# Attention logits, exponentials and the byte mask of a two-layer graph network: from VectorE by tiles to ScalarE by heads, with other positions of the steps

## The chip, the core and the metric

The kernel runs on one core of one Trainium2 chip. The metric is the device time of one execution in microseconds (us); less is better. The engines are TensorE (PE, with its weight loads PEld), VectorE (DVE), ScalarE (ACT), GpSimd (POOL) and SyncE (SP), which here issues every DMA. Each engine has its own queue of instructions, in the order in which the program gives them; between engines, semaphores make one wait for another.

## What is computed

```python
# layer 0: 12 heads of 64, 128 graphs of 64 nodes, 768 features
h = einsum('bnd,ade->bane', x, W);  th = tanh(h)
attn = (th @ w_src) + swapaxes(th @ w_dst, 2, 3)
attn = where(attn >= 0, attn, 0.2 * attn)          # the leaky unit
attn = softmax(where(~adj, -999.0, attn), axis=-1)
f = elu(attn @ h + b);  gate = sigmoid(x @ H_w.T + H_b)
x = layernorm(x + gate * f + (1 - gate) * x)
# layer 1: 6 heads of 128, masked softmax attention with Wq, Wk, Wv, Wf
x = layernorm(x + attention(x, adj))
```

All is float32; the adjacency is bytes.

## The kernel before

**Tiles and pairs.** The 8192 nodes are 64 tiles of 128 rows (two graphs each), worked on in 32 pairs. Of a pair, `t1` is the second tile and `t0` the first; keys in the tables of positions end in 1 or 0 for them.

**Items.** Layer 0 is one long list of items, and each item is one product on PE. `a0` to `a14` are the fifteen products (L925) by which a pair's features and gate are made (a fast matrix multiplication with fifteen in place of eighteen block products, each of two chunks and 512 columns). `v1` to `v7` are the seven products of layer 1's values (L962), one pair behind; written `u` they belong to the pair before that. From the fifth pair on every pair has the same 22 items, the table `TURN`; such a stretch is called a turn here. The first four pairs have their own tables `EARLY`, and `LAST` ends the phase.

**Ways out.** A product adds into a bank of PSUM, its path (`PRODUCTS`, L49). A path is used by several products, and the bank is read between them: `step` (L369) first gives PE the product and then writes out the product before it (`way_out`, L948), either by a copy or a negation on ACT where a block of `hg` is written for the first time, or by an addition on DVE. The next product of the same path has to wait until that read is done: a12 uses the same path as a10, with one item between them, and a14 the same as a12.

**Positions.** All other work is entered in a plan at positions counted in items (the tables `NEW`, `SUMS` and `OLD`, those with `EARLY` for the first four pairs). After each item the plan's steps of that position are emitted in order of their positions (L1344 to L1350). `behind_of` (L1263) counts from the last of some of the pair's products, `was` (L1257) from the beginning of the next turn for the tile's later steps, `at` (L1260) from the beginning of the pair's own turn. The product a7 stands at item 11 of a turn, a14 at 17, a12 at 15, before and after. So a position on an engine is only its place in that engine's queue.

**The steps of one tile's attention**, in order:

- `products` (L975, key tanh): tanh on ACT, then th times the two vectors on DVE (L980) and POOL (L981)
- `terms` (L984): the sums over 64 features on DVE (L989), giving `sd`, 24 numbers a row; a transpose on DVE (L994)
- `send` (L997) and `fetch` (L1000): the transposed terms go to DRAM and come back as `dd`, spread over the rows of each graph; SP issues one DMA and then two
- `with_bias`, `other_half` (L1009, L1016; keys bias and hx): a bias on POOL, two DMAs that swap the halves
- `logits` (L1023): one DVE addition over 128x768 with `sd` spread over the columns; `leaky` (L1034): one ACT instruction over 128x768
- `masked` (L1038): DVE replaces masked places by -999 (L1042), takes each head's maximum (L1048) and subtracts it (L1049)
- `exps` (L1051): one ACT instruction over 128x768, which writes the heads in the order in which PE turns them
- `probs_by_nodes` (L1069, key probs): PE turns prob into two banks, ACT copies them out (L1067)
- `attend` (L1080): 48 small products, `av`; `features` (L1096): reciprocals and products on DVE, then an exponential on ACT (L1111)
- `elu1`, `gated` (L1119, L1124): three DVE operations, the last at L1130; `stats`, `power`, `normed`: the layernorm's sums on DVE, the root on POOL, the result on ACT

`mask` (L1176) makes, once a pair, bytes that are 1 where there is no edge. `gate_bias` on POOL (L1185) and `gate_tanh` on ACT (L1187) prepare the gate, and `residual` (L1114) multiplies on POOL. `x_sums` (L868) makes the next operands on POOL.

**Weights.** Products read their weights from slots of `wa`, one a product. While the last pair runs, slots that are done with are filled with layer 1's weights for queries and keys (`load_wide`, L447); `wide_place` (L438) says which slot, by the constant `ORDER`, which lists the products in the order in which `TURN` uses them. From the fourth pair to the last, one more stream of DMAs and POOL operations makes sums of layer 1's weights (`sum_weights`, L410).

**Layer 1** (L1361 on) has its own loops and is not touched by the change.

Of the kernel before, what the change touches and what calls it, by code (L numbers as in the profile page):

```python
# [16 lines left out]
P = 128  # L17
N = 64
# [53 lines left out]
ORDER = (0, 1, 5, 3, 8, 6, 7, 2, 10, 9, 12, 4, 14, 11, 13)  # L72
# [60 lines left out]
TURN = "u6 a0 a1 u5 u7 a5 a3 u4 u3 a8 a6 a7 a2 a10 a9 a12 a4 a14 a11 v1 a13 v2".split()  # L133

EARLY = (
    "a0 a5 a1 a7 a3 a8 a6 a10 a9 a2 a12 a4 a11 a14 a13".split(),
    "a0 a5 a3 a7 a8 a6 a1 a9 a10 a2 a12 a4 a11 a14 a13".split(),
    "a0 a1 a3 a5 a8 a6 a7 u1 u2 u6 u5 u7 a10 u4 a2 a9 a12 a11 a4 a14 a13 u3".split(),
# [4 lines left out]
NEW = dict(tanh1=1, terms1=3.3, bias1=3.7, send1=6.3, hx1=4.6, fetch1=6.5, logits1=8.5, leaky1=10.5,  # L143
    masked1=10.8, exps1=11, tanh0=1.6, terms0=3.3, bias0=3.4, send0=4.2, hx0=6.8, fetch0=4.6,
    gbias0=3.7, gbias1=2.8)
SUMS = dict(next6=2.1, next9=0.4, next2=2, next3=2.6, next0=2.7, next5=9.9, next8=5.9, own10=4.3, own12=5.8,
    own13=1.6)
OLD = dict(probs1=4.7, gtanh1=1.7, resid1=3.2, attend1=5.3, feat1=5.5, elu1=6, gated1=7.7, stats1=8.2, pow1=9,
    norm1=10.6, byf1=12.3, spill1=13.7, logits0=1.3, leaky0=2.5, masked0=3.6, exps0=5, gtanh0=6.9,
    resid0=7.7, probs0=7.8, attend0=10.5, feat0=11, elu0=12, gated0=13.8, stats0=14, pow0=14.9,  # L150
    norm0=16.6, byf0=17.3, spill0=20.7, sum0=17.9, sum1=18.3, sum2=23, sum3=28, spillT=21.5, spillV=12,
    mask=7.7, adj=6.4, xT=2.7, inputs1=0.8, inputs0=17.3, plus1=13.7, plus0=19.7)
OLD_EARLY = [
    dict(probs1=1.5, gtanh1=0, resid1=2.5, attend1=3, feat1=4.7, elu1=6, gated1=6.1, stats1=7, pow1=8,
        norm1=9.3, byf1=10, spill1=13, logits0=3, leaky0=4.3, masked0=5, exps0=5.7, gtanh0=4.5,
        resid0=5.8, probs0=8, attend0=11, feat0=12, elu0=12.2, gated0=13.6, stats0=14, pow0=15,
        norm0=15.5, byf0=17.5, spill0=18, sum0=10.4, sum1=18, sum2=20.7, sum3=26.9, spillT=19,
        spillV=11, mask=6, adj=3, xT=-2, inputs1=9.2, inputs0=14.5, plus1=14.9, plus0=17.5),
    dict(probs1=-3.3, gtanh1=1, resid1=1.5, attend1=3, feat1=4.7, elu1=5.7, gated1=7.1, stats1=7.3,
        pow1=8, norm1=9, byf1=11.3, spill1=11.7, logits0=2.5, leaky0=4, masked0=5, exps0=6.3,  # L160
        gtanh0=2.2, resid0=6.8, probs0=8, attend0=10, feat0=10.5, elu0=12, gated0=12.4, stats0=13,
        pow0=14, norm0=16, byf0=17, spill0=22.5, sum0=12, sum1=18, sum2=22, sum3=23.7, spillT=19.5,
        spillV=13, mask=6.5, adj=5.2, xT=-3, inputs1=10.5, inputs0=12.7, plus1=14.3, plus0=15),
    dict(probs1=2.5, gtanh1=1, resid1=3.5, attend1=4.5, feat1=5, elu1=6, gated1=6.1, stats1=9, pow1=9.5,
        norm1=11, byf1=11.3, spill1=12, logits0=1.7, leaky0=4.6, masked0=5, exps0=6, gtanh0=1.5,
        resid0=2.1, probs0=8.3, attend0=10, feat0=11, elu0=11.7, gated0=13.1, stats0=13.3, pow0=14,
        norm0=15, byf0=16.3, spill0=17, sum0=12, sum1=18, sum2=20.5, sum3=21, spillT=19, spillV=14,
        mask=4, adj=-0.3, xT=-0.6, inputs1=10.5, inputs0=13.2, plus1=13.7, plus0=17),
    dict(probs1=1.5, gtanh1=1, resid1=2, attend1=3.5, feat1=4.5, elu1=6, gated1=6.1, stats1=6.7, pow1=8,
        norm1=9, byf1=10, spill1=12.3, logits0=3, leaky0=4, masked0=4.5, exps0=6.5, gtanh0=1.7,  # L170
        resid0=5.7, probs0=8, attend0=9, feat0=10, elu0=12, gated0=12.1, stats0=14, pow0=15, norm0=16,
        byf0=17, spill0=19, sum0=11, sum1=18.5, sum2=22, sum3=23, spillT=18.5, spillV=11.6, mask=8.2,
        adj=2.5, xT=1.3, inputs1=13, inputs0=12, plus1=14.6, plus0=16.7),
]
NEW_EARLY = [
    dict(tanh1=1, terms1=2, bias1=3.1, send1=3.5, hx1=5.3, fetch1=6, logits1=8, leaky1=9, masked1=10,
        exps1=12, tanh0=1.3, terms0=2.5, bias0=3.1, send0=4, hx0=4.7, fetch0=5.7, gbias0=1, gbias1=1.5),
    dict(tanh1=1, terms1=3, bias1=2.5, send1=4, hx1=4.5, fetch1=4.5, logits1=8.3, leaky1=9.5,
        masked1=10, exps1=10.5, tanh0=2, terms0=3.2, bias0=2.9, send0=4.6, hx0=3, fetch0=7.5, gbias0=1,
        gbias1=7),  # L180
    dict(tanh1=1, terms1=2, bias1=4.6, send1=3.8, hx1=7, fetch1=6, logits1=7.7, leaky1=9.3,
        masked1=10.3, exps1=11, tanh0=1, terms0=2, bias0=3.1, send0=4.2, hx0=7.5, fetch0=9.5, gbias0=1,
        gbias1=1.6),
    dict(tanh1=1.3, terms1=3, bias1=3.6, send1=4, hx1=5, fetch1=4.5, logits1=8, leaky1=8.4, masked1=9.7,
        exps1=10.5, tanh0=1, terms0=2.2, bias0=6.4, send0=4, hx0=7, fetch0=6.3, gbias0=1.3, gbias1=1.3),
]
SUMS_EARLY = [
    dict(next6=0, next9=1.1, next2=1.5, next3=1.6, next0=4.9, next5=2.5, next8=1, own10=1.5, own12=0.9,
        own13=1),
    dict(next6=1.3, next9=0.1, next2=0.9, next3=1.6, next0=3.4, next5=0.8, next8=0.5, own10=2,  # L190
        own12=2.6, own13=1.5),
    dict(next6=0.8, next9=1.1, next2=2.2, next3=2.3, next0=3.6, next5=1.5, next8=3, own10=2.1,
        own12=0.1, own13=1),
    dict(next6=1, next9=1.1, next2=1.2, next3=1.3, next0=1.4, next5=1.5, next8=2.7, own10=1, own12=3.1,
# [5 lines left out]
def kernel(  # L200
# [236 lines left out]

    def wide_place(key, n):  # L438
        if key == "f":
            flat, at = weights[key].rearrange("p b k f -> p (b k f)"), PLACE[n]  # L440
        else:
            i = n + (key == "k") * NW
            flat, at = weights["a"].rearrange("p b k f -> p (b k f)"), 2 * ORDER[i // 2] + i % 2
        at = at * 2 * W2
        return flat[:, at : at + 2 * W2].rearrange("p (k f) -> p k f", k=2)
# [373 lines left out]
    with ExitStack() as ph, ExitStack() as ph_r:  # L819
# [203 lines left out]
        def logits(t):  # L1023
            sd, dd = st[t].pop("sd"), st[t].pop("dd")
            att = work(f"att_{t}")
            V.tensor_tensor(  # L1026
                att.rearrange("p (a c m) -> p a c m", c=2, m=32),
                dd.rearrange("p (c a m) -> p a c m", c=2, m=32),
                sd[:, H0 : 2 * H0].unsqueeze(2).unsqueeze(3).to_broadcast([P, H0, 2, 32]),
                ALU.add,  # L1030
            )
            st[t]["att"] = att

        def leaky(t):  # L1034
            att = st[t]["att"]
            S.activation(att, att, AF.Prelu, alpha=LEAKY)

        def masked(t):  # L1038

            att = st[t]["att"]  # L1040
            att3 = att.rearrange("p (a m) -> p a m", m=N)
            V.copy_predicated(  # L1042
                att3,
                st[t]["nadj"].unsqueeze(1).to_broadcast([P, H0, N]),
                neg0.unsqueeze(1).to_broadcast([P, H0, N]),
            )
            mx = small.tile([P, H0], F32, tag="mx", name=f"mx_{t}")
            V.tensor_reduce(mx, att3, AX.X, ALU.max)  # L1048
            V.tensor_tensor(att3, att3, mx.unsqueeze(2).to_broadcast([P, H0, N]), ALU.subtract)  # L1049

        def exps(t):  # L1051

            att = st[t].pop("att")
            prob = work(f"prob_{t}")
            S.activation(
                prob.rearrange("p (j a m) -> p a j m", a=2, m=N),
                att.rearrange("p (a j m) -> p a j m", a=2, m=N),
                AF.Exp,
            )
            st[t]["prob"] = prob  # L1060
# [115 lines left out]
        def mask(p):  # L1176
            ad = adjs.pop(p)
            na = sb.tile([P, PAIR, N], U8, tag="nadj", name=f"nadj_{p}", bufs=2)
            V.tensor_scalar(na, ad, 0, None, ALU.is_equal)
# [69 lines left out]
        for p in range(NP + 1):  # L1249
# [10 lines left out]
            def at(pos, *acts):  # L1260
                put(new_at[p] + pos, *acts)
# [4 lines left out]
            if q >= 0:  # L1266
# [7 lines left out]
                for key, f in (("logits", logits), ("leaky", leaky), ("masked", masked), ("exps", exps)):  # L1274
                    was(old[key + "0"], do(f, t0))
# [25 lines left out]
            for n, i in ((n1, "1"), (n0, "0")):  # L1301
                put(old_at[q] + old["inputs" + i] if p else 8, do(inputs, n))
                put(old_at[q] + old["plus" + i] if p else 14, do(plus_one, n))
                for key, f in (
                    ("tanh", products), ("terms", terms), ("bias", with_bias), ("send", send), ("hx", other_half),
                    ("fetch", fetch), ("logits", logits), ("leaky", leaky), ("masked", masked), ("exps", exps),
# [7 lines left out]
            if p == NP - 1:  # L1314

                at(4, do(load_wide, "q", wq, range(4)))
                at(8, do(load_wide, "q", wq, range(4, 8)))
                at(13, do(load_wide, "q", wq, range(8, NW)))
                at(13, do(load_wide, "k", wk, range(1)))
                at(15, do(load_wide, "k", wk, range(1, 5)))  # L1320
                at(17, do(load_wide, "k", wk, range(5, 9)))
# [188 lines left out]
```

## Time and profile before

| what | value |
| --- | --- |
| three runs | 2906.47, 2908.09, 2908.53 us; median 2908.09 |
| the profiled execution | 2907.37 us |
| its span, first to last instruction | 2905.6 us |
| mean granted TensorE clock | 0.995 |
| ACT idle in front of `exps` (L1055), waiting for L1049 | 154.7 us, 32 times |
| DVE idle in front of `logits` (L1026), waiting for dd | 99.6 us, 59 times |
| dd<-dstd: median from issue to landing | 4.0 us |
| dstd<-sdT: median from issue to landing | 1.7 us |

A line of a group of instructions reads: line, engine, operation, tile written <- tiles read, shapes, count | busy us, mean ns of one | idle time of the engine just in front of them, and what ended it. In a line of a stretch stand, after its bounds, its length and then the busy us of PE, PEld, DVE, ACT and POOL with counts, the granted clock, the share of the DMA engines and GB/s. A line of the timeline gives start, us, engine and instruction; instructions that run on are merged, and idle time in front stands in brackets. A wait is put down to the semaphore that came last by the profile; where that one had long come, another one is meant.

### The profile page before, as it was taken

To read this page: it belongs to the slowest core of one execution; us is meant where nothing else is said; L and a number is where in the kernel's file an instruction comes from. 1 tells how busy PE (TensorE), PEld (TensorE's weight loads), DVE (VectorE), ACT (ScalarE), POOL (GpSimd) and SP (SyncE) were. 2 spreads that over 40 slices of the span, in tenths; PEclk is the share of its full clock that TensorE was granted. 3 is DMA by queue.
4 is the path that set the end of the run, shared out by engine and by line. 5 is a ranking of instruction groups with operands and counts; after the bars stand their busy time and mean duration, and the time that the engine had idled before them with its cause. 6 is when DMAs were issued, how large, how long until landed. Compare 5 with 4: busy or idle time off the path is not lost. (4 is left out here: it accounts for less than half of the span.)

```text
span 2905.6 us, 46458 instructions
## 1 busy us (share of the span) xinstructions
PE 2813.2 (97%) x17484; PEld 1926.9 (66%) x17484; DVE 1999.5 (69%) x3282; ACT 1105.0 (38%) x1961; POOL 1547.2 (53%) x1501
## 2 busy tenths in 40 slices
PE   7899999999999999999999999999999999999998
PEld 3444554545444454545558888888888888888886
DVE  8868888888887888888874445555545555554556
ACT  3444544445444444444443123333223333322332
POOL 5546666666666666565544454434545443444534
PEclk9999999999999999999999999999999999999999
DMA  5344454444445354433452434332333433233332
GB/s 184 118 142 140 141 160 130 154 146 150 144 136 163 124 157 137 134 119 104 138 180 84 129 110 110 106 92 70 85 88 110 110 101 89 71 84 96 110 88 73
DMA packets 321439, 349.08 MB, mean 120 GB/s; under 512 B 145728, under 2 KB 249152, under 8 KB 321216
## 3 DMA queue, kind: packets, MB, share of 16 engines
q1 hardware_dynamic: 321216, 346.11, 38.7%
q8 instruction: 139, 2.28, 0.3%
q14 instruction: 84, 0.69, 0.1%
HBM read 198.48 MB, written 122.95 MB: 111 GB/s over the span
## 5 line engine op out<-in xcount | busy, mean ns | idle before, releaser
L939 PE MATMUL y_a<-wa,sx 128*128 128x512 f32 x1024 | 482.5, 603 | 45.0 <-POOL sd L988 23.9
L939 PEld LDWEIGHTS y_a<-wa,sx 128*128 128x128 f32 x1024 | 188.2, 191 | 255.8 <-issue 159.8
L1117 POOL TENSOR_TENSOR x<-hg,x 128x768 f32<-128x768 f32 x64 | 138.1, 2158 | 249.8 <-ACT hg L1191 249.8
L758 POOL TENSOR_TENSOR y<-y,bf_bc 128x768 f32<-128x768 f32 x64 | 114.6, 1812 | 290.0 <-issue 236.2
L637 ACT ACTIVATE sc<-sc 128x512 f32<-128x512 f32 x48 | 30.7, 639 | 614.9 <-DVE sc L634 614.9
L981 POOL TENSOR_TENSOR th<-th,wsd 128x768 f32<-128x768 f32 x64 | 135.9, 2123 | 213.9 <-DVE th L980 209.8
L570 DVE TENSOR_TENSOR y<-y,z_o 128x256 f32<-128x256 f32 x320 | 127.3, 417 | 139.7 <-PE z_o L557 139.5
L557 PE MATMUL z_o<-wf,so 128*128 128x256 f32 x896 | 215.8, 383 | 2.3 <-DVE y L570 1.2
L510 PE MATMUL z_q<-xs,wa 128*128 128x256 f32 x896 | 213.0, 381 | 0.4 <-POOL x L1117 0.4
L474 POOL TENSOR_TENSOR so<-ctxT 128x256 f32<-128x256 f32 x224 | 159.8, 730 | 90.6 <-PE y_o L557 46.1
L386 POOL TENSOR_TENSOR rs_b<-ve_b,minus_half 128x1 f32<-128x1 f32 x64 | 40.4, 631 | 313.6 <-DVE ve_b L384 312.8
L510 PE MATMUL z_k<-xs,wa 128*128 128x256 f32 x840 | 198.5, 379 | 0.0
L939 PE MATMUL z_a<-wa,xT 128*128 128x512 f32 x384 | 185.5, 606 | 4.8 <-DVE wa L862 3.2
L557 PEld LDWEIGHTS z_o<-wf,so 128*128 128x128 f32 x896 | 167.2, 190 | 26.9 <-issue 2.0
L510 PEld LDWEIGHTS z_q<-xs,wa 128*128 128x128 f32 x896 | 168.9, 190 | 24.1 <-POOL x L1117 0.8
L510 PEld LDWEIGHTS z_k<-xs,wa 128*128 128x128 f32 x840 | 159.5, 190 | 21.7
L955 DVE TENSOR_TENSOR hg<-hg,y_a 128x512 f32<-128x512 f32 x225 | 151.4, 674 | 24.0 <-PE y_a L939 20.2
L1026 DVE TENSOR_TENSOR att<-dd,sd 128x768 f32<-128x768 f32 x64 | 95.4, 1490 | 99.6 <-DMA dd<-dstd 99.6
L525 DVE TENSOR_TENSOR qT<-qT,z_q 128x512 f32<-128x512 f32 x96 | 65.9, 687 | 141.0 <-PE z_q L510 141.0
L474 POOL TENSOR_TENSOR xs<-r,r 128x512 f32<-128x512 f32 x112 | 146.7, 1326 | 25.5 <-PE y_k L510 12.5
L1154 ACT ACTIVATE x<-x,sh_a,rs_a 128x768 f32<-128x768 f32 x64 | 65.7, 1027 | 239.6 <-DVE sh_a L1153 239.6
L334 PE MATMUL y_v<-wv,sv_v 128*128 128x384 f32 x384 | 139.1, 500 | 12.7 <-ACT v L970 12.6
(156 smaller groups left out, 6558.2 us busy)
## 6 DMA issues: line engine op xcount, KB each, us to landing
xT<-in_xT_dram SPq DMA_DIRECT2D x32, 768.0 KB, 6.4
x<-in_x_dram SPq DMA_DIRECT2D x64, 384.0 KB, 4.7
dd<-dstd SPq DMA_DIRECT2D x128, 192.0 KB, 4.0
x1d<-x SPq DMA_DIRECT2D x64, 384.0 KB, 4.1
x1Td<-x1T SPq DMA_DIRECT2D x32, 768.0 KB, 3.7
vd<-v SPq DMA_DIRECT2D x64, 384.0 KB, 3.0
r<-x1Td SPq DMA_DIRECT2D x96, 256.0 KB, 3.0
v<-vd SPq DMA_DIRECT2D x384, 64.0 KB, 2.2
```

Source lines behind the costliest of these rows:

```text
L334: T.matmul(to[:, : self.n], lhsT, rhs, start=kc == 0 and not more, stop=kc == HK - 1, skip_group_check=more,)
L474: G.tensor_tensor(t, self.of(x[0]), self.of(x[2]), x[1])
L510: T.matmul(b[:, half * W2 : (half + 1) * W2], w[:, kc, half * P : (half + 1) * P], x[:, kc, :], start=half == kc == 0 and not more, stop=k ...
L525: V.tensor_tensor(at, at, b.rearrange("p (h t) -> p h t", h=2), ALU.add if sign > 0 else ALU.subtract,)
L557: T.matmul(b[:, :W2], x[:, kc, :], w[:, kc, :], start=kc == 0 and not more, stop=kc == 1, skip_group_check=more,)
L570: V.tensor_tensor(at, at, self.banks[path][:, :W2], ALU.add if sign > 0 else ALU.subtract)
L758: G.tensor_tensor(y, y, pools["bf"], ALU.add)
L939: T.matmul(b, x[:, kc, :], wa[:, n, kc, :], start=kc == 0 and not more, stop=kc == 1, skip_group_check=more,)
L955: V.tensor_tensor(at, at, b, ALU.add if sign > 0 else ALU.subtract)
L981: G.tensor_tensor(th[:, 1, :], th[:, 1, :], wsd[:, 1, :], ALU.mult)
L1026: V.tensor_tensor(att.rearrange("p (a c m) -> p a c m", c=2, m=32), dd.rearrange("p (c a m) -> p a c m", c=2, m=32), sd[:, H0 : 2 * H0].un ...
L1117: G.tensor_tensor(xp, gate_of(t), xp, ALU.mult)
```

## The change

`logits` no longer adds on VectorE: for each of six heads one ScalarE instruction over 128x64 takes `dd`, adds the head's column of `sd` as its bias and applies the leaky unit. The other six heads follow in `more_logits`, at the positions that `leaky` had. `masked` gives the maximum with its sign turned and subtracts nothing; `exps` is twelve ScalarE instructions a tile, each with the head's column of the negated maximum as its bias. `mask` is a ScalarE instruction (one minus the byte) in place of a VectorE comparison.

```diff
         def logits(t):
             sd, dd = st[t].pop("sd"), st[t].pop("dd")
             att = work(f"att_{t}")
-            V.tensor_tensor(
-                att.rearrange("p (a c m) -> p a c m", c=2, m=32),
-                dd.rearrange("p (c a m) -> p a c m", c=2, m=32),
-                sd[:, H0 : 2 * H0].unsqueeze(2).unsqueeze(3).to_broadcast([P, H0, 2, 32]),
-                ALU.add,
-            )
+            dd3 = dd.rearrange("p (c a m) -> p a c m", c=2, m=32)
+            att3 = att.rearrange("p (a c m) -> p a c m", c=2, m=32)
             st[t]["att"] = att
-        def leaky(t):
-            att = st[t]["att"]
-            S.activation(att, att, AF.Prelu, alpha=LEAKY)
+            def heads(which):
+                for a in which:
+                    S.activation(
+                        att3[:, a], dd3[:, a], AF.Prelu, bias=sd[:, H0 + a : H0 + a + 1], alpha=LEAKY
+                    )
+            heads(range(H0 // 2))
+            st[t]["more_heads"] = lambda: heads(range(H0 // 2, H0))
+        def more_logits(t):
+            st[t].pop("more_heads")()
...
-            V.tensor_reduce(mx, att3, AX.X, ALU.max)
-            V.tensor_tensor(att3, att3, mx.unsqueeze(2).to_broadcast([P, H0, N]), ALU.subtract)
+            V.tensor_reduce(mx, att3, AX.X, ALU.max, negate=True)
+            st[t]["mx"] = mx
         def exps(t):
-            att = st[t].pop("att")
+            att, mx = st[t].pop("att"), st[t].pop("mx")
             prob = work(f"prob_{t}")
-            S.activation(
-                prob.rearrange("p (j a m) -> p a j m", a=2, m=N),
-                att.rearrange("p (a j m) -> p a j m", a=2, m=N),
-                AF.Exp,
-            )
+            for a in range(H0):
+                at = 2 * (a % J0) + a // J0
+                S.activation(
+                    prob[:, at * N : (at + 1) * N],
+                    att[:, a * N : (a + 1) * N],
+                    AF.Exp,
+                    bias=mx[:, a : a + 1],
+                )
...
-            V.tensor_scalar(na, ad, 0, None, ALU.is_equal)
+            S.activation(na, ad, AF.Identity, bias=one, scale=-1.0)
```

The items of a turn stand in another order, and the constant `ORDER` is gone: the slots follow from `TURN` itself (`used`), and a group of the wide weights' loads is entered one item behind the last use of its slots.

```diff
-TURN = "u6 a0 a1 u5 u7 a5 a3 u4 u3 a8 a6 a7 a2 a10 a9 a12 a4 a14 a11 v1 a13 v2".split()
+TURN = "u6 a1 u5 a0 u7 a5 a3 u3 a8 u4 a6 a7 a9 a10 a2 a12 a4 a14 a11 v1 a13 v2".split()
...
+    used = [int(item[1:]) for item in TURN if item[0] == "a"]
...
-            flat, at = weights["a"].rearrange("p b k f -> p (b k f)"), 2 * ORDER[i // 2] + i % 2
+            flat, at = weights["a"].rearrange("p b k f -> p (b k f)"), 2 * used[i // 2] + i % 2
...
-                at(4, do(load_wide, "q", wq, range(4)))
...
+                    last = used[(ns[-1] + (key == "k") * NW) // 2]
+                    put(at_of[p, last] + 1, do(load_wide, key, src, ns))
```

Most positions change, in the tables of the early pairs too. The main ones of the turns (the counts begin as told above):

| step | before | after |
| --- | --- | --- |
| terms1, bias1, send1, hx1, fetch1 | 3.3, 3.7, 6.3, 4.6, 6.5 | 3.1, 5.5, 7.5, 8.6, 8.7 |
| logits1, leaky1, masked1, exps1 | 8.5, 10.5, 10.8, 11 | 9.3, 10, 10.3, 12.5 |
| terms0, bias0, send0, hx0, fetch0 | 3.3, 3.4, 4.2, 6.8, 4.6 | 4, 4.9, 4.2, 5.7, 4.3 |
| logits0, leaky0, masked0, exps0 | 1.3, 2.5, 3.6, 5 | 2, 3.1, 3.7, 5 |
| probs1, attend1, probs0, attend0 | 4.7, 5.3, 7.8, 10.5 | 3.3, 5, 8, 10.5 |
| gated0, stats0, norm1, norm0 | 13.8, 14, 10.6, 16.6 | 12.3, 14, 10.1, 16.1 |
| mask, gbias1, gbias0, gtanh1 | 7.7, 2.8, 3.7, 1.7 | 5.9, 1.8, 5.8, 0.5 |

## The prediction

> **What bounds the kernel now.** I read the page's busy shares first, then one turn of layer 0 by windows, then what TensorE waited for, then the timeline around its gaps.
>
> ```profile
> PE 2813.2 (97%) x17484; PEld 1926.9 (66%) x17484; DVE 1999.5 (69%) x3282; ACT 1105.0 (38%) x1961; POOL 1547.2 (53%) x1501
> 1333.27:1378.86 45.59, 44.54 (x222) 23.07 (x223) 38.38 (x57) 21.58 (x34) 25.97 (x25) 1.00 0.35 115
> 914.65:965.57 50.92, 46.89 (x222) 23.73 (x223) 39.30 (x57) 21.36 (x34) 30.16 (x29) 0.97 0.43 138
> 1496.72:2905.60 1408.88, 1393.09 (x10554) 1199.16 (x10554) 743.27 (x1494) 429.89 (x892) 644.77 (x670) 1.00 0.34 95
> ```
>
> TensorE (PE) sets the end: it is busy 97%. The second line is an undisturbed turn, a12 to a12: 45.59 us with 44.54 of PE, so 1.05 us idle, while VectorE (DVE) has 38.4 and ScalarE (ACT) 21.6. The third is the worst turn. From 224.40 to 1470.03 there are 27 turns, 46.13 us on average: 0.54 above the quiet one. After 1496.7 nearly all is layer 1, which the edit does not touch. So at most 27 x (1.05 + 0.54) = 43 us lie in the turns, and some 20 in the four early pairs and the last one.
>
> ```profile
> PE y_a L939 <- POOL sd L988: 23.9, 23, 1.5
> PE y_v L334 <- ACT v L970: 12.6, 4, 5.0
> PE y_a L939 <- DVE hg L955: 11.1, 24, 1.7
> ...
> 1378.86 1.10 PE L939 MATMUL y_a<-wa,sx 128*128 128x512 f32 x2 [0.89 <-POOL sd L988]
> ...
> 1373.80 0.96 DVE L980 TENSOR_TENSOR th<-th,wsd 128x768 f32<-128x768 f32 x1
> 1374.68 0.95 DVE L1128 SCALAR_TENSOR_TENSOR ex<-hg,ex 128x768 f32<-128x768 f32 x1
> 1375.66 2.45 DVE L1130 TENSOR_TENSOR x<-ex,x 128x768 f32<-128x768 f32 x1
> 1378.04 0.67 DVE L955 TENSOR_TENSOR hg<-hg,y_a 128x512 f32<-128x512 f32 x1
> ...
> 1374.84 2.46 POOL L981 TENSOR_TENSOR th<-th,wsd 128x768 f32<-128x768 f32 x1 [4.82 <-DVE th L980]
> ```
>
> The page names GpSimd's `sd`, a memset that ended at 1378.75; but a12 also waits on DVE, whose L955 ended at 1378.71. That L955 is a10's way out, from the bank that a12 adds into. It was late because L1130 took 2.45 us (the turn's other one 0.96) beside GpSimd's L981, which took 2.46. This 0.89, with 0.15 before a14, is the idle time of every turn.
>
> ```profile
> 1491.06 0.84 ACT L1055 ACTIVATE prob<-att 128x768 f32<-128x768 f32 x1 [4.72 <-DVE att L1049]
> 1491.81 0.46 ACT L970 COPY v<-y_v 128x384 f32<-128x384 f32 x1
> ...
> 1492.32 4.21 PE L334 MATMUL y_v<-wv,sv_v 128*128 128x384 f32 x6 [4.66 <-ACT v L970]
> ...
>   DMA dd<-dstd: 99.6, 59
> ```
>
> The large gaps have one shape. DVE waits for dd to land (the last line, asked at L1026: 59 waits, 1.7 us each), then masks late; ACT stands at `exps`, and the copy of a PSUM bank is queued behind it. The granted clock stood at 0.5 for 6.8 us from 1490.9: those six matmuls took 4.21 us instead of 2.10.
>
> **The change, part by part**, per turn (two tiles).
>
> ```profile
> L1026 DVE TENSOR_TENSOR att<-dd,sd 128x768 f32<-128x768 f32 x47 | 71.8, 1528 | 78.9 <-DMA dd<-dstd 78.9
> L1049 DVE TENSOR_TENSOR att<-att,mx 128x768 f32<-128x768 f32 x47 | 57.9, 1232 | 1.6
> L1179 DVE TENSOR_SCALAR nadj<-adj 128x128 uint8<-128x128 uint8 x24 | 39.4, 1642 | 0.0
> ...
> 2009.89 0.63 ACT L637 ACTIVATE sc<-sc 128x512 f32<-128x512 f32 x1
> 2010.41 1.13 ACT L669 COPY scT<-sc 128x512 uint16<-128x512 uint16 x2
> ...
> 2028.67 1.56 ACT L723 ACTIVATE ctxT<-cp,bv_c 128x256 f32<-128x256 f32 x4
> ```
>
> (The first three lines are groups from 200 to 1300 us: busy, mean ns of one.)
>
> *Removed from DVE:* 2 x 1.53 (L1026), 2 x 1.23 (L1049), 1.64 (L1179): 7.2 us, so 38.4 falls to 31.2. Writing the maximum negated costs nothing more (the same reduce).
>
> *Added on ACT:* 24 instructions of 128x64 with a bias column in each tile, for two of 128x768. No row has that shape. Overlapped, a 128x512 takes 0.52 (2009.89 to the next start at 2010.41), a 128x768 0.75 (1491.06 to 1491.81): 0.90 ns an element, 0.12 at 64. The column adds 0.09 (L1111 with one averages 0.935, L1055 without 0.844): 0.21 us. Bounds: 0.12, if the column hides too; 0.37, if nothing overlaps (durations 0.639 at 512 and 0.844 at 768 give 0.28, plus 0.09). L723's four in 1.56 us overlap, so I take 0.21. Per turn 2 x (24 x 0.21 - 2 x 0.75) = +7.1; the mask on ACT lies between 0.15 (0.12 and 64 more elements) and 0.42, taken as 0.27. ACT rises to about 29 of 45 us; at 0.37 to 36. It is the bound in neither case: the question is what its queue holds back.
>
> The Trainium skill (ScalarE: Activation LUTs, What ACT_TABLE_LOAD costs) gives 280 ns + 0.833 ns an element with a bias column, and 93 ns of overlap back to back: estimated 0.24 us for 64, so +8.5 instead of +7.1. No run here shows it at this width; L1111's 0.935 agrees at 768 within 2%. By it the slacks below shrink by 0.4 us and the sum stays.
>
> *The chains.* Time 0 is the start of a12 at 1378.86; times of before are from the timeline of the turn that follows, positions count items from the pair's own turn. For tile 1, dd landed at 9.7. Six heads then take to 11.0, the other six to 12.3, DVE's mask and maximum (1.08 + 0.95) to 14.5. `exps` sits at 23.5, behind `gtanh` and u6's copy, whose bank PE leaves near 15.5; it runs 16.0 to 18.6. PE turns prob behind a0 (`probs1` 4.7 to 3.3, one v product earlier): about 20.7. Slack 2 us; before, prob was there at 18.0 for 22.8. For tile 0, dd landed at 20.2; DVE no longer stands at L1026 ahead of the reduce, so I take 19.5. Then 12 heads to 22.0 and, queued behind them on ACT, tile 1's two pT copies (0.86) to 22.9; `attend1` needs them near 24.8. Slack 1.9. At 0.37 both slacks are used up.
>
> *a12's gap.* `gated0` goes from 13.8 to 12.3, ahead of `tanh1`, so L1130 runs before L980 releases L981: 0.96 instead of 2.45. The same four DVE operations still stand ahead of a10's way out; the work taken off DVE lies elsewhere in the turn and gives nothing here. a2, written by ACT, now stands between a10 and a12 as a9 did. From av's end to a12 is 7.6 us against 7.7. I leave 0.35 of 1.05: 27 x 0.7 = -19. Bounds: -28 (all of 1.05 x 27), 0 (L1130 is slowed by another GpSimd operation).
>
> *Irregular excess* (27 x 0.54 = 15 us): DVE is free for its reduce while dd is under way; but ACT now waits for dd itself. Half comes back: -7. Bounds -15 and +15 (it doubles).
>
> *New waits* at pT or av: 0.2 a turn, +5 (bounds 0 and the rival's).
>
> *Early pairs and the last:* some 23 us of gaps (1.7 at 66.8, 1.9 at 75.8, 4.3 at 93.8, 5.0 at 189.6, 4.7 at 1492.3 and small ones). All positions there move, without a rule that I can price: -4, between -15 (two thirds close) and +10 (the five grow by 2 each).
>
> *SP's and GpSimd's queues:* no DMA more or less. `hx1` moves from ahead of `send1` to behind it (15.6 to 19.6, two issues, 1.0 us). GpSimd's `bias1` goes from 14.7 to 16.5; hidden in the 1.75 us that SP waits for send to land, but a late `bias1` now delays tile 1's fetch. `fetch1` goes from 17.5 to 19.7 and `logits1` from 19.5 to 20.3, so ACT can stand at dd; v1's copy was queued ahead, v2 is read by DVE, u6's copy is due near 15.5. The wide weights' loads come one item after each slot's last use: the same issues, hidden before layer 1.
>
> Sum: -19 - 7 + 5 - 4 = -25. The profiled execution took 2907.37 (span 2905.6, 1.8 around it), 0.7 under the median: 2907.4 - 25 = 2882, and 2883 for the median.
>
> **The rivals.**
> *Deeper (0.16).* Every DVE-made gap closes: -28 - 15 - 10 gives about 2855. For it: DVE has 14 us free. Against: ACT's order is strict and its blocks longer.
> *Nothing moves (0.12).* DVE's load was not what PE waited for; only L1130's place was, and another GpSimd operation slows it there. Within 0.2% (2902 to 2914; about what measurement here can tell from no change).
> *Slower (0.26): ACT is late for `attend1`.* PE waits at av for pT copies queued behind tile 0's heads. It decides from dd0 landing plus 12 heads plus 0.86 passing 24.8: with 0.37 a head and 20.2, 25.5 is 0.7 late; with dd 1 us later, as when weight-sum DMAs share SP (the turn at 914.65), 1.7. At 1.6 us a turn, near the second, 27 x 1.6 = +43, less 19 from a12: 2931. For it: PE has already waited for pT at av three times (3.7 us in all). Against: ACT is under two thirds busy.
> The Trainium skill (ScalarE: Activation LUTs, Rules for kernel authors) says to put add, mul and max on VectorE, which speaks for this rival; the rows agree, 24 x 0.21 on ACT a tile for 2.76 taken off DVE.
>
> **How the numbers follow.** Forecast (0.46): 2883, by itself 2866 to 2900. The deeper case reaches down to 2852, the slower up to 2932; 8 in 10 lie in 2855 to 2928. Faster 0.62, same 0.12, slower 0.26.
>
> **What would show it.** Right: a12 stalls under 0.4 us a turn, L1130 near 0.96, heads 0.2 us apart, ACT 29 a turn, DVE 31. Wrong: heads 0.3 apart or more, or PE waits at pT and av over 0.5 us a turn.

## The result and the profile after

| | before | after |
| --- | --- | --- |
| median of four runs each, on one chip | 2907.28 us (2904.97 to 2908.53) | 2867.27 us (2866.45 to 2868.03) |
| span of the profiled execution | 2905.6 us | 2864.4 us |

The ratio is 0.9863 [0.9846, 0.988]: 1.4% faster, 40 us by the medians. The first view is a table by stretches: bounds, length, busy us of PE, PEld, DVE, ACT and POOL, clock, DMA share, GB/s. First the kernel before: its four early pairs (to the first product of pair 5) and its 27 turns. PE's column against the length is what to look at.

```profile
0.00:193.60 193.60, 162.66 (x702) 78.51 (x703) 156.31 (x219) 74.06 (x113) 99.92 (x102) 0.97 0.45 152
193.60:1440.00 1246.40, 1206.65 (x5996) 623.39 (x5995) 1055.09 (x1508) 575.79 (x917) 778.03 (x709) 1.00 0.43 138
```

The same two stretches of the changed kernel, then its last pair and one undisturbed turn, a14 to a14:

```profile
0.00:190.57 190.57, 161.26 (x703) 77.80 (x704) 141.53 (x201) 106.18 (x273) 98.41 (x102) 0.98 0.46 154
190.57:1400.99 1210.42, 1201.94 (x5995) 623.10 (x5994) 896.21 (x1374) 809.93 (x2121) 695.15 (x708) 1.00 0.43 142
1400.99:1454.13 53.14, 48.52 (x236) 25.16 (x234) 37.93 (x56) 36.97 (x105) 22.39 (x22) 0.99 0.71 230
1344.64:1389.27 44.63, 44.41 (x222) 23.07 (x222) 32.88 (x53) 30.06 (x79) 22.23 (x25) 1.00 0.35 117
```

The 27 turns give 36.0 of the 41.2 us that the span lost, the early pairs 3.0, the last pair 3.6 (56.72 before); layer 1 takes 1.4 more (1410.3 after 1408.9). In the turns length less busy PE is PE's idle time: 1246.40 - 1206.65 = 39.8 before, 1210.42 - 1201.94 = 8.5 after. So 31.3 of the 36.0 are waits that are gone, and 4.7 is PE being busy for less. ACT does 234 us more in the turns than before and DVE 159 less, and neither figure by itself explains 36.

What PE waited for inside the turns, by the list of waits (us in total, times, longest), in the kernel before:

```profile
PE y_a L939 <- POOL sd L988: 23.9, 23, 1.5
PE y_a L939 <- DVE hg L955: 7.1, 18, 1.7
PE av L1087 <- ACT pT L1067: 3.7, 3, 1.4
PE y_v L334 <- ACT v L970: 3.0, 2, 1.6
```

and after, the whole list:

```profile
PE y_a L942 <- DVE hg L958: 7.1, 28, 0.6
PE x1Tp L1076 <- ACT x L1164: 1.4, 1, 1.4
```

The 23.9 at a12, which the page puts down to GpSimd's memset, is gone, and so are the waits for ACT's copies. L958 (L955 before) is the addition by which DVE writes a product out; it now holds up only a14. The timeline around a12 and a14 of an undisturbed turn of the changed kernel shows why (start, us, engine and line):

```profile
1337.75 1.38 DVE L1140 TENSOR_TENSOR x<-ex,x 128x768 f32<-128x768 f32 x1
1339.05 0.94 DVE L983 TENSOR_TENSOR th<-th,wsd 128x768 f32<-128x768 f32 x1
1339.91 0.68 DVE L958 TENSOR_TENSOR hg<-hg,y_a 128x512 f32<-128x512 f32 x1
...
1337.58 0.73 POOL L880 TENSOR_TENSOR sx<-xT,sx 128x256 f32<-128x256 f32 x1 [3.11 <-PE y_a L942]
1340.07 1.81 POOL L984 TENSOR_TENSOR th<-th,wsd 128x768 f32<-128x768 f32 x1 [1.76 <-DVE th L983]
...
1340.74 1.95 PE L942 MATMUL y_a<-wa,sx 128*128 128x512 f32 x4
```

L1140 (L1130 before) now runs ahead of L983, so GpSimd's long L984 starts only when both are over. a10's way out ends at 1340.59, and a12 follows the product before it without a gap. What the turn still loses is 0.23 in front of a14. DVE still has a long wait beside GpSimd, at a place where it does no harm: ten us earlier tile 1's L1140 took 2.25 (from 1327.50) beside GpSimd's L1127, where the L1130 of tile 1 in the quiet turn of before took 0.96, and PE waits for neither.

ACT's queue in the turn from 1296.09 on (the start of its a12) answers the prediction's chains:

```profile
1306.70 2.97 ACT L1035 ACTIVATE att<-dd,sd 128x64 f32<-128x64 f32 x12
1312.69 2.98 ACT L1064 ACTIVATE prob<-att,mx 128x64 f32<-128x64 f32 x12
1316.45 2.97 ACT L1035 ACTIVATE att<-dd,sd 128x64 f32<-128x64 f32 x12 [0.30 <-DMA dd<-dstd]
1319.33 0.83 ACT L1077 COPY pT<-pTp 128x384 f32<-128x384 f32 x2
```

Twelve heads take 2.97 us and one lasts 0.334 (the group's mean), so the next comes (2.97 - 0.33) / 11 = 0.24 us later. ACT stood at dd for 0.30 in this turn; the pT copies queued behind the heads ended at 24.1 on the prediction's clock, and PE took them at 25.4.

### The profile page after: what moved, and what is told of

It is laid out like the page before. It is cut to its first block, busy times and chain, and to the rows that moved or that the text cites. A ratio compares the mean times of both kernels' runs of the same rounds, so it can differ in the third digit from the quotient of the medians.

```text
span 2864.4 us, 47725 instructions
## 1 busy us (share of the span) xinstructions
PE 2807.1 (98%) x17484; PEld 1926.9 (67%) x17484; DVE 1817.2 (63%) x3122; ACT 1385.5 (48%) x3401; POOL 1460.9 (51%) x1501
## 5 line engine op out<-in xcount | busy, mean ns | idle before, releaser
L1127 POOL TENSOR_TENSOR x<-hg,x 128x768 f32<-128x768 f32 x64 | 112.5, 1759 | 197.3 <-ACT hg L1201 197.3
L984 POOL TENSOR_TENSOR th<-th,wsd 128x768 f32<-128x768 f32 x64 | 117.8, 1840 | 180.1 <-DVE th L983 180.1
L958 DVE TENSOR_TENSOR hg<-hg,y_a 128x512 f32<-128x512 f32 x225 | 153.0, 681 | 85.7 <-PE y_a L942 82.4
L1035 ACT ACTIVATE att<-dd,sd 128x64 f32<-128x64 f32 x768 | 191.0, 335 | 32.9 <-DMA dd<-dstd 32.6
L1064 ACT ACTIVATE prob<-att,mx 128x64 f32<-128x64 f32 x768 | 190.3, 334 | 22.3 <-DVE mx L1055 20.7
L1049 DVE COPY_PREDICATED_SCALAR att<-nadj,neg 128x768 f32 x64 | 68.4, 1069 | 153.5 <-ACT att L1035 153.4
```

The costliest lines, as they stand in the source:

```text
L958: V.tensor_tensor(at, at, b, ALU.add if sign > 0 else ALU.subtract)
L984: G.tensor_tensor(th[:, 1, :], th[:, 1, :], wsd[:, 1, :], ALU.mult)
L1035: S.activation(att3[:, a], dd3[:, a], AF.Prelu, bias=sd[:, H0 + a : H0 + a + 1], alpha=LEAKY)
L1049: V.copy_predicated(att3, st[t]["nadj"].unsqueeze(1).to_broadcast([P, H0, N]), neg0.unsqueeze(1).to_broadcast([P, H0, N]),)
L1064: S.activation(prob[:, at * N : (at + 1) * N], att[:, a * N : (a + 1) * N], AF.Exp, bias=mx[:, a : a + 1],)
L1127: G.tensor_tensor(xp, gate_of(t), xp, ALU.mult)
```

## The experiments

Four theories were set against each other. **A**: the places in the queues carry the gain, and slacks of one to two us hide ACT's longer blocks. **B**: the load taken off DVE carries it. **C**: it is DVE no longer standing at `logits` for dd. **D**: every microsecond taken off DVE counts, in proportion. The runs that lengthen ACT's blocks ask besides whether time put on ACT is paid for. In an expectation, a letter means what stands beside it there. Every ratio below is against the kernel before, run on the same chip.

**Positions alone, and the code alone.** The change was cut in two. The first run has the new order of items and all new positions, with the three parts of the old code put back: the mask on DVE, `logits` as a DVE addition with one leaky ACT instruction, and the subtraction with one exponential a tile:

```diff
-            S.activation(na, ad, AF.Identity, bias=one, scale=-1.0)
+            V.tensor_scalar(na, ad, 0, None, ALU.is_equal)
...
+            V.tensor_tensor(
+                att.rearrange("p (a c m) -> p a c m", c=2, m=32),
+                dd.rearrange("p (c a m) -> p a c m", c=2, m=32),
+                sd[:, H0 : 2 * H0].unsqueeze(2).unsqueeze(3).to_broadcast([P, H0, 2, 32]),
+                ALU.add,
+            )
...
-            heads(range(H0 // 2))
-            st[t]["more_heads"] = lambda: heads(range(H0 // 2, H0))
...
-            V.tensor_reduce(mx, att3, AX.X, ALU.max, negate=True)
+            V.tensor_reduce(mx, att3, AX.X, ALU.max)
+            V.tensor_tensor(att3, att3, mx.unsqueeze(2).to_broadcast([P, H0, N]), ALU.subtract)
```

> The new order and positions with the old code: logits, maximum subtracted and mask on VectorE by tiles, one leaky unit and one exponential a tile on ScalarE. Theory A (positions and their order on VectorE made the gain, as the prediction's a12 term has it): the gap before a12 stays under 0.4 us, a turn is 44.7 to 45.3 us, the time 2870 to 2890. Theory B (the 7 us a turn taken off VectorE made it): the gap before a12 is back at 0.9 or more, VectorE stands at dd again, a turn is 45.6 or more, the time 2900 to 2920.

Measured: 2884.33 us, 0.9904 [0.9885, 0.9922]; the 27 turns took 1221.0, a quiet one 44.66, the early pairs 199.8. A quiet turn is as short as that of the changed kernel (44.64), so its gain comes from the positions and the order alone. What the code adds lies elsewhere: the excess of the mean turn over the quiet one is still 0.56 here, as before, and 0.19 in the changed kernel, and the early pairs take 190.6 there.

The second run is the reverse: the kernel before, its positions and its order of items, with the new code of all three parts (the signs of the diff turned round).

> The old order and positions with the new code (heads and mask on ScalarE). Theory A: the gap before a12 stays near 0.9 us, since the same four VectorE operations stand ahead of a10's way out; a turn 45.3 to 45.8 us, the time 2890 to 2910. Theory B: VectorE is free earlier, the gap closes, a turn is 44.8 us, the time 2868 to 2880.

Measured: 2935.43 us, 1.0086 [1.0067, 1.0106], slower than any theory had it. Its waits of PE (the longest three of the list):

```profile
PE y_a L939 <- POOL sd L988: 21.2, 23, 1.5
PE y_v L334 <- ACT v L970: 19.4, 13, 4.9
PE av L1094 <- ACT pT L1074: 14.4, 21, 0.9
```

The first row is the old gap at a12: taking the work off DVE did not touch it. The third is the place of the rival "ACT is late for `attend1`", with 21 waits instead of 3, and the second is PE behind the copies of v, 13 times instead of 4 over the whole run, which are queued on ACT between its blocks. So the rival's mechanism is real; the new positions keep it away. Positions alone gain 28 us (0.0096 of 2907), the code alone loses 25, both together gain 40: at the new positions the code is worth 12. B falls as the main cause.

**Which positions.** Two of them (`tanh1` is not in the table of main positions), put into the kernel before, and then taken back from the changed kernel:

```diff
-NEW = dict(tanh1=1, ...
-    ... gated0=13.8, ...
+NEW = dict(tanh1=1.7, ...
+    ... gated0=12.3, ...
```

> The kernel before with two positions of the turns changed: gated0 from 13.8 to 12.3 and tanh1 from 1 to 1.7, so that the last operation of gated comes ahead of the product of tanh that releases GpSimd. Theory A: L1130 takes 0.96 to 1.4 us there in place of 2.45, the gap before a12 falls from 0.9 to 0.0 to 0.4, the time is 2880 to 2893 (27 turns by 0.6 to 1.0). Theory B: the gap stays, 2900 to 2912.

Measured: 2900.39 us (ten runs, 2893.81 to 2908.58), 0.9965 [0.9953, 0.9976], so 10 us faster. The time misses A's range by 7 us and lies at the lower edge of B's, but the gap at a12 closed, as A has it, and quiet turns took 44.4 to 44.6. It was the mean turn, 45.7, that was longer: over the whole run PE's wait behind the copies of v rose from 12.6 us to 24.3 (16 times), that for pT from 3.7 to 5.5. Nearly two thirds of the some 28 us (27 x 1.05) that the two positions free was lost again in irregular turns, 1.2 x 27 = 32 us of excess instead of 15; in the whole change it is kept.

The same diff with its signs turned, in the changed kernel:

> The changed kernel with the same two positions as before (gated0 13.8, tanh1 1). Theory A: the operation again takes some 2.4 us beside GpSimd, a gap of 0.6 to 1.0 us opens before a12 in every turn, the time is 2883 to 2895. Theory B: no gap, since VectorE is lighter; 2866 to 2872.

Measured: 2904.65 us (ten runs), 0.9976 [0.9965, 0.9987]. The timeline around a12 of one of its turns:

```profile
681.09 2.45 DVE L1140 TENSOR_TENSOR x<-ex,x 128x768 f32<-128x768 f32 x1
683.46 0.68 DVE L958 TENSOR_TENSOR hg<-hg,y_a 128x512 f32<-128x512 f32 x1
...
680.26 2.45 POOL L984 TENSOR_TENSOR th<-th,wsd 128x768 f32<-128x768 f32 x1 [3.34 <-DVE th L983]
...
684.28 1.96 PE L942 MATMUL y_a<-wa,sx 128*128 128x512 f32 x4 [1.34 <-DVE hg L958]
```

L1140 is back at 2.45 beside L984, and a12 waits for a10's way out again. The wait is 1.34 us, more than the 0.6 to 1.0 expected, and the time lies 10 us above A's range; DVE also stands 0.43 at ACT's tanh ahead of these operations. With some 5 us less work on DVE in a turn, these two positions alone are worth 0.9976 - 0.9863 = 0.0113, 33 us, where they were worth 10 in the kernel before. That is theory A at its plainest.

**Each part of the code undone alone**, in the changed kernel, by the three parts of the first diff.

The mask:

> The changed kernel with only the byte mask back on VectorE (1.64 us a turn there, some 0.3 less on ScalarE). With the positions kept, all three old parts together cost some 12 us. Theory C (what the heads give is that VectorE no longer stands at dd, which only the logits do): nothing, ratio to before 0.984 to 0.989. Theory D (every us taken off VectorE counts, in proportion): 1.64 of 7.16, about +3 us, ratio 0.987 to 0.990.

Measured: 2868.23 us, 0.9849 [0.9834, 0.9863], inside C's range and below D's.

The logits:

> The changed kernel with only the logits back on VectorE by tiles and one leaky unit at the place of the second half. Theory C: VectorE stands at dd again ahead of its other work; nearly all of the 12 us is lost, ratio 0.989 to 0.992. Theory D: 3.06 of 7.16, about +5 us, ratio 0.987 to 0.989.

Measured: 2870.94 us, 0.9856 [0.9841, 0.9871], below C's range and at the lower edge of D's. DVE stood at dd for 120.3 us, 57 times (99.6 and 59 in the kernel before).

The exponentials:

> The changed kernel with only the maximum subtracted on VectorE again and one exponential a tile. ScalarE has 4.2 us a turn less, VectorE 2.5 more. Theory C: nothing, ratio 0.984 to 0.988. Theory D: 2.46 of 7.16, about +4 us, ratio 0.987 to 0.989. If ScalarE's load were what limits the changed kernel, it would be faster, ratio under 0.984.

Measured: 2878.29 us, 0.988 [0.9865, 0.9894]; its turns took 1216.5 (+6.1), its early pairs 196.1 (+5.5). C's range and D's meet here, and the ratio fits both.

None of the three can be told from the changed kernel by its ratio, whose interval is [0.9846, 0.988]. C falls: with DVE standing at dd again the turns took 1209.8 us against 1210.4. D does not show for the mask either, and for the logits at most at its edge. For the exponentials the trace points to some 10 us, which the intervals leave open.

**The slack of ACT's blocks.** Each exponential was run once more, beside the first, writing the same again:

```diff
-            for a in range(H0):
+            for a in [i for i in range(H0) for _ in range(2)]:
```

> The changed kernel with each of the twelve exponentials run twice over the same output: 12 more instructions at 0.239 us, 2.9 us in each tile. In the quiet turn of the changed kernel tile 1's prob is done at 19.5 us behind the start of a12 and TensorE turns it at 20.9: slack 1.4. If that chain is the nearest edge, as the rival of the prediction has it, 2.9 less 1.4 is lost in every turn: a wait of 1.5 us at pTp, 28 turns, +42 us, 2900 to 2920. If ScalarE has more room than that, under +10 us.

Measured: 3122.82 us, 1.0721 [1.0703, 1.0739], a turn 52.54: far beyond both. The experiment did not measure what it was meant to. A pair took 0.62 us, not 2 x 0.24, since the second, which rewrites the first one's output, waited for a semaphore that the first raises; so 4.6 us came on top for each tile, not 2.9. It was repeated with the two rounds apart, and with four heads only:

```diff
-            for a in range(H0):
+            for a in [*range(H0), *range(H0)]:
+            for a in [*range(4), *range(H0)]:
```

> The changed kernel with the twelve exponentials run through twice, one round after the other, so that no instruction waits for the one just before it: 12 x 0.239 = 2.9 us in each tile (with pairs side by side it was 4.6, since the second of a pair waited for the first). Theory A: tile 1 is 2.9 - 1.4 late and TensorE loses 1.0 to 1.5 us at pTp; tile 0 is late by twice 2.9 less what TensorE has lost and less 3.3, 1.0 to 1.5 again; a turn 46.7 to 47.6, ratio 1.003 to 1.014. Theory B: both tiles lose all of it, a turn 50 or more, ratio over 1.03.

Measured: 3009.08 us, 1.0339 [1.0321, 1.0356], a turn 49.14, between the two theories. With 2.9 us more a tile, PE was done with tile 1's prob 1.0 us late, not 2.9 - 1.4 = 1.5. Its six transposes stood 0.24 apart, as the heads do, instead of 0.11, so PE took each pair of heads as it came; the last transpose, which alone needs all heads, stands 0.5 behind the first, and 2.9 - 1.4 - 0.5 = 1.0. The prediction's slack of 2 gives nearly the same, but it was not worked out that way. The turn grew by 4.5, above A's 2 to 3: PE also waited 1.43 a turn for ACT's copy of a product queued behind the exponentials, and 0.47 for the transposes of x1, which come after the layernorm.

> The changed kernel with four exponentials of each tile run once more ahead of the twelve: 4 x 0.24 = 1.0 us more on ScalarE in each tile's chain. Theory A (the chain from exponentials to TensorE's turning of prob has 1.4 us of slack for tile 1, as the changed kernel's timeline shows, and some 3 for tile 0): no loss, a turn 44.6 to 44.9, ratio 0.984 to 0.990. Theory B (ScalarE has no slack, as the large loss with every exponential twice could also mean): 2 us a turn lost, ratio 1.003 or more.

Measured: 2893.41 us, 0.9939 [0.992, 0.9959], a quiet turn 45.36 (+0.72), between the two theories. Here 0.96 us came on top for each tile, inside both slacks of the prediction, and neither was touched: PE turned prob at 21.0 and began av at 25.4, as in the changed kernel. The loss was elsewhere. PE began to turn x1 of tile 1 at 39.02 instead of 38.81, once the layernorm's last instruction on ACT was over (994.85 + 1.03 = 995.88), and took 0.92 instead of 0.65 for it:

```profile
994.85 1.03 ACT L1164 ACTIVATE x<-x,sh_a,rs_a 128x768 f32<-128x768 f32 x1 [2.94 <-DVE sh_a L1163]
...
995.93 0.94 PE L1076 MATMUL x1Tp<-ident,x 128*128 128x128 f32 x6
```

So the nearest edge of the changed kernel is a chain that no step of the prediction names: `exps0`, the exponential of `features`, `elu1` to `normed1`, the transposes of x1. Followed matmul by matmul, PE lags by 0.21 us at the first of these transposes, by 0.48 behind the last, by some 0.6 at the second matmul of the product that follows, and by the whole 0.72 from the next a12 on. So at most 0.4 of the 0.96 added was slack here, worked out from one run. Up to that edge time on ACT is hidden: the heads and the exponentials, 2.97 us each a tile, cost a quiet turn nothing (44.64, and 44.66 with the old code at the same positions). Beyond it time on ACT costs nearly in proportion: from four exponentials more to twelve more, 3.8 us were added in a turn and 3.8 lost.

**The exponentials' new form at the old positions**: the kernel before with the third part of the change alone.

```diff
-            V.tensor_reduce(mx, att3, AX.X, ALU.max)
-            V.tensor_tensor(att3, att3, mx.unsqueeze(2).to_broadcast([P, H0, N]), ALU.subtract)
+            V.tensor_reduce(mx, att3, AX.X, ALU.max, negate=True)
...
+            for a in range(H0):
...
+                    bias=mx[:, a : a + 1],
```

> The kernel before, at its own positions, with only the maximum's subtraction replaced by twelve exponentials with bias columns. All new parts together at these positions cost 25 us. Theory A (long blocks on ScalarE hold back the copies queued behind them, at y_v and av): some of that loss is here, ratio 1.001 to 1.008, with TensorE waiting for the copies of v and pT. Theory B (the subtraction on VectorE is the costly part at any positions, as it was with the new ones): faster, ratio 0.994 to 0.998.

Measured: 2905.35 us (ten runs), 0.9981 [0.9971, 0.999]; the turns of the profiled execution, one of the slower of the ten (2907.37), took 1246.3, as before. It costs nothing even there: A's expectation was wrong, and B's is met at its edge, though with 5 us, little. By difference, the 25 us that the whole code costs at the old positions come with the logits on ACT, with the mask, or with all three parts together. The logits were not tried alone there, so this is argued and not shown; a likely way is that ACT's first six heads stand at dd at the early position of `logits`, with copies of PSUM behind them.

**A version beyond both.** What is left in the changed kernel's turn is 0.23 us in front of a14: on DVE, tile 1's 1.75 us sum over features and the 0.21 us transpose stand ahead of a12's way out. The transpose became a step of its own, placed behind that way out in the turns:

```diff
+        def turned(t):
...
-            V.transpose(sdT, sd)
+            V.transpose(sdT, st[t]["sd"])
...
+            new = dict(new, turned0=new["terms0"], turned1=5.05 if 4 <= p < NP - 1 else new["terms1"])
```

> The changed kernel with VectorE's transpose of the terms taken out of that step and, for tile 1 in the turns, put behind a12's way out (position 5.05 in place of 3.1): what stands ahead of that way out gets 0.2 to 0.3 us shorter. Theory A: the last gap of a turn, 0.23 us before a14, falls to 0.0 to 0.1, and tile 1's chain, 0.7 us later, still fits its 1.4 us of slack: a turn 44.45 to 44.55 in place of 44.64, 2.5 to 5 us in all, ratio 0.984 to 0.987. Theory B: tile 1's dd comes later than its slack, a wait at pTp or av takes the place, a turn 44.8 or more.

Measured: 2860.62 us (2858.03 to 2861.35), 0.9827 [0.9811, 0.9844]; span 2856.0, a quiet turn 44.33. Its timeline before a14:

```profile
1293.14 0.68 DVE L958 TENSOR_TENSOR hg<-hg,y_a 128x512 f32<-128x512 f32 x1
1293.73 0.20 DVE L999 STREAM_TRANSPOSE sdT<-sd 128x32 f32<-128x32 f32 x1
...
1293.87 1.98 PE L942 MATMUL y_a<-wa,xT 128*128 128x512 f32 x4
```

The bracket of idle time in front of a14 is gone. The interval lies just under that of the changed kernel, and the span is 8.4 us shorter: the best version of this study, about 1.7% under the kernel before. It did better than A had it (0.984 to 0.987), though of the 8.4 us 1.5 lie in layer 1, which the edit does not touch.

## Why the prediction was right, and by how much it was short

**What bounds it.** Held: PE is busy 98%, and the time came out of the turns, 36 of 41 us, and of their gaps.

**Prices.** A head costs 0.24 us in line, not 0.21, and the mask's instruction lasts 0.387, inside its bounds. ACT has 30.1 us a turn (29 forecast), DVE 32.9 (31.2 forecast). DVE's 7.2 removed was too much for a quiet turn: the means from 200 to 1300 us contain the slowed instances, and in the quiet turn of before the five instructions took 2.2, 2.0 and 1.7, together 5.9; the quiet turn lost 5.5 of DVE's time in all. For a head, the price carried down from rows of 512 and 768 elements was 0.03 low, over 48 heads 1.4 us a turn. The estimate by the Trainium skill (ScalarE: Activation LUTs, What ACT_TABLE_LOAD costs) was 0.24, and the rows agree.

**The chains.** The forecast had tile 1's prob turned at 20.7 and tile 0's copies done at 22.9; they came at 21.0 and 24.1, later by about the dearer heads and because dd of tile 0 let ACT go at 20.4, where I had taken 19.5. PE was not there earlier either (25.4 for av against 24.8), so slacks of 1.4 and 1.3 remained where 2 and 1.9 were forecast.

**The terms of the sum**, 25 forecast against 41 measured:

| term | forecast | measured |
| --- | --- | --- |
| gaps at a12 and a14, 1.05 a turn | -19 | -22 (0.23 left: 27 x 0.82) |
| irregular excess in the turns | -7 | -10 (0.57 to 0.19 a turn) |
| new waits at pT or av | +5 | none in the list |
| early pairs and the last | -4 | -6.6 |
| PE's own time in a quiet turn | not in it | -3.5 (44.54 to 44.41) |
| layer 1 | 0 | +1.4 |

The mechanism of the first term was right. One detail was not: L1140 took 1.38 and not 0.96, since it now stands beside GpSimd's `x_sums`; that is short enough. Its size was too small, because the prediction counted idle time alone. PE's own time in a quiet turn goes with the gap at a12, and not with the order of the products: it is 44.54 with the gap in the old order (before), 44.41 without it in the new one (after), and these are quiet turns of the new order with the gap (the two positions taken back) and of the old order without it (the two positions in the kernel before):

```profile
1250.26:1296.32 46.06, 44.55 (x223) 23.06 (x222) 33.97 (x51) 30.07 (x80) 23.57 (x25) 1.00 0.34 113
1198.55:1242.98 44.43, 44.30 (x224) 23.14 (x222) 36.95 (x57) 21.36 (x34) 24.34 (x25) 1.00 0.37 118
```

So the two rows of the table belong together: -26 (27 x 0.95) for the -19 forecast, the term that was mis-sized most. Next is "New waits at pT or av: 0.2 a turn, +5", which charged for a slack that was not used up. With the irregular excess (two thirds came back, not half) and the early pairs, less the 1.4 of layer 1, it makes the 16 us.

The size of the irregular excess came near, but the reason given for it is not what the runs show, so that term was partly luck. The prediction had DVE free for its reduce while dd is under way. With the logits back on DVE, which then stood at dd for 120.3 us, the turns took no longer (1209.8); with the positions alone the excess stayed, and of the parts of the code only the exponentials undone brought some of it back (6.1 us). How they do it stays open.

Of the stretches at half clock before, those at 94.8 and 944.7 us (3.4 us each) have no counterpart after, and the waits ahead of them (4.3 us, and 1.6 and 1.4 us) are gone too. The one at the end of the last pair (6.8 us from 1490.9) now lies almost wholly in layer 1 (6.8 us from 1453.1), so some of the last pair's gain is layer 1's loss; a new one stands at the end of layer 1 (from 2859.4).

**The rivals.** The time lies between the forecast and "Deeper", a little nearer the latter's 2855, and what "Deeper" had for it is what happened: nearly every DVE-made gap in the turns closed. It did not get there because 0.23 stayed before a14 and the early pairs kept 29.3 us of idle time (30.9 before). "Nothing moves" is out: the two positions move L1140, and the run with them taken back is at 0.9976. "Slower" has its mechanism shown, at the old positions: there pT is late 21 times. Its rule, dd's landing plus twelve heads plus 0.86 passing 24.8, gave 24.1 here. The rule that speaks for it in the Trainium skill (ScalarE: Activation LUTs, Rules for kernel authors: add, mul and max on VectorE) agrees with the code alone, +25 us, and not with the whole change: with the queues laid out anew, the same code gains some 12 us.

## What to carry to other kernels

Where two engines stall each other, look first at the order in their queues: two steps exchanged around the DVE instruction that releases GpSimd were worth 33 us here (10 in the kernel before, where other waits took most of it back), and 5 us a turn less work on DVE did nothing for that gap. Work that is moved to another engine needs positions that go with it: the same code cost 25 us at the old ones and gained 12 at the new ones; at the old ones PE waited 14.4 us for pT copies queued on ACT behind the heads, and 3.7 before. Before calling a chain safe, lengthen it in small steps on the chip: the edge that gave way first was one that had not been listed.

## What the hardware did that was not expected

**DVE does not slow down beside GpSimd, it waits for it.** The prediction took L1130's 2.45 us for a slowed instruction. But it ends a constant 0.8 us after GpSimd's: in the kernel before L981 ended at 1374.84 + 2.46 = 1377.30 and L1130 at 1378.11; after, L880 at 1338.31 and L1140 at 1339.13; with the two positions back, L984 at 682.71 and L1140 at 683.54. Of L1140's 64 instances in the trace of after, 58 began under a GpSimd instruction and all of them ended 0.81 or 0.82 us behind it; the other six took 0.95 or 0.96. GpSimd waits likewise: its L981 and L984 took 2.46 and 2.45 where they began under a DVE instruction that reads two tiles (L1128, L1138), and 1.81 where they began under the addition of a bank of PSUM (L955, L958). DVE's mask over bytes took 1.70 in 27 of its 32 instances, which ended 0.08 or 0.09 behind GpSimd's L1117, and 0.22 to 0.25 in four others, which is why its mean of 1.64 was no price of its own. The Trainium skill (SBUF — State Buffer, SBUF: two separate sides) describes the port pair of the two engines as "an exclusive lock, not a bandwidth split", held for its whole instruction by whoever starts first, and counts a DVE instruction with two inputs in SBUF among its takers when GpSimd reads SBUF; the rows of L1130 and L1140 agree.

**Two ACT instructions in line that write the same place were held apart by a semaphore.** In the run with each exponential doubled, the second of a pair carries a wait for the semaphore that the first raises, and it began 0.03 us after the first one's end: the pair took 0.62 us where two that write different places take 0.48. So this wait stands in the program, and no run shows what the engine would do without it. Anyone who lengthens a chain by running things twice must keep the copies apart.
